# A graph network's steady loop: a new table of due times, and the output bias moved from TensorE to GpSimd

## The chip, the cores and the metric

The kernel runs on one core of a Trainium2 chip. Its engines work beside each other, each through its own list of instructions in a fixed order, and wait for each other by semaphores: TensorE (PE, with its weight loads listed as PEld), VectorE (DVE), ScalarE (ACT), GpSimd (POOL) and SyncE (SP), which issues the transfers. The metric is the device time of one execution in microseconds (us); of several runs the median is taken.

## The reference

Two layers over 128 graphs of 128 nodes with 64 features, each followed by a residual addition and a layer norm. Layer 0 sums a relu over the edges that exist, layer 1 is a dense product with the adjacency followed by three small linear layers.

```python
# layer 0
mask = (adj > 0.0).astype(x.dtype)
h = relu((x @ W1a)[:, :, None, :] + (x[:, :, None, :] - x[:, None, :, :]) @ W1b + b1)
hm = einsum('bjkh,bjk->bjh', h, mask)
x = layernorm(x + hm @ W2 + mask.sum(-1)[..., None] * b2)
# layer 1
h = elu(einsum('bmn,bnd->bmd', adj, x) @ V1 + c1)
h = elu(h @ V2 + c2)
x = layernorm(x + h @ V3 + c3)
```

H is 192 in layer 0, 128 in layer 1; about 6% of the adjacency is nonzero.

## The kernel before

Two graphs make a pair; there are 64 pairs, and every step below works on one pair. The nodes of a graph are sorted by degree, so that nodes with few edges stand together. The sorted nodes fall into nine blocks (`BLOCKS`), each with a number of slots that no node of the block is expected to exceed. For each block, a *unit* computes the edge sums: ACT fills a PSUM bank with the node's own term (L910, "fill"), PE adds the neighbours' terms through a one-hot matrix `oh` (18 matmuls at L920, "gather"), DVE sums absolute values over the slots (L930, "reduce"). Four PSUM banks (`edges`) serve the units in turn. A second path, at the end of the program, handles pairs with too many edges; no instruction of it appears among the costly groups.

Before its units a pair is prepared. `prepare` counts degrees (DVE L545), forms keys (POOL L552, L553), spreads them over the partitions (PE L248, "spread") and ranks the nodes (DVE L568, L575). `turn` transposes inputs (PE L690, L691; ACT L695). `project_c` forms the neighbours' projection in three bf16 parts, `cp` (PE L708, L711; ACT L718; DVE L722; ACT L725; POOL L727). `sort_x` and `project_a` sort the features and form the own term `aj` (PE L592 "x sort", L606 "projection a"; ACT L613), and a correction `corr` (POOL L620 `sa`; PE L626, L629 "short rows"; DVE L635 `ea`; POOL L642). `sort_mask` sorts the mask (PE L246 "mask sort"; ACT L659, L661), takes prefix sums ("vps"; ACT L668) and writes the one-hot matrices, nine per pair (DVE L675).

After its units a pair is finished by `finish`: POOL `hm` (L842), PE "project" (L847, L851), ACT `ys` (L855), PE "unsort" (L864), then `norm`, giving `x1` (DVE L737 addition and L742 statistics; POOL L749, L750, L753, called "fac1" here; ACT L771), PE "aggregate" (L871), ACT `agg` (L875), PE "hidden1" (L880), `elu` (ACT r L791, e L794; DVE h L797), PE "hidden2" (L886), `elu` again, PE "last" (L891 and L893), and `norm` again ("fac2" is its POOL part), giving `o`, which SP writes out (L897). In the old kernel L891 adds the bias row `c3` by a matmul of ones with `rowp`, in which the row stands as three bf16 parts, in front of the two products L893 that accumulate onto it. The row was centred when it was prepared (`consts_late`, a chain of some twenty small DVE operations, L508 to L366), since the norm subtracts the mean.

What order the instructions stand in is decided when the program is built, by `Flow`. Each activity above is a thread, a list of steps, and each step has a due time: `ROUND` times the pair's number plus an entry of `DUE`. At first, `Flow.run` issues whatever its cost estimates say can start earliest. From the first fill on (`flow.under_way`), and until the last 14 units, it issues in strict order: of all threads whose next step has its inputs issued and PSUM banks free, the one with the smallest due time. Apart from units, the other steps share four further PSUM banks, handed out in the order in which they were given back. The due times thus are ranks: they set the order on every engine, and no engine ever passes an instruction that waits. Where PE changes between full-array matmuls and tiled ones the planner also distinguishes modes (`PE:t` two column halves, `PE:r` two row halves, `PE:x` transposes).

Of the kernel before, what the change touches and what calls it, by code (L numbers as in the profile page):

```python
# [31 lines left out]
F32 = mybir.dt.float32  # L32
# [154 lines left out]
def sparse(tc, env):  # L187

    g = type("env", (), dict(env))
    nc, P, N, F, H, O, HB, H1, NP, E = (  # L190
        g.nc, g.P, g.N, g.F, g.H, g.O, g.HB, g.H1, g.NP, g.E)
# [7 lines left out]
    EV = {}  # L199


    ROUND = 11.1651
    AHEAD = 4

    DUE = {
        "prepare": (-42.67, -37.79, -37.67, -37.41, -37.15),
        "sort_x": (-21.11, -18.03, -15.85, -13.03, -12.9, 2.76, 2.89, 3.02, 3.14),
        "sort_mask": (-28.04, -27.66, -27.27, -15.21, -14.95, -14.31, -14.05, -13.8, -13.54,
                      -13.28, -3.02, -2.76, -2.5, -2.25),
        "turn": (-38.05, -37.92),  # L210
        "project_c": (-31.63, -29.71, -29.58, -29.45, -29.32, -17.13, -13.15),
        "finish": (12.51, 20.73, 21.24, 21.37, 21.5, 21.88, 22.01, 27.91, 28.3, 28.68, 32.02,
                   34.97, 35.1, 35.23, 41.26, 41.39, 43.95, 44.08, 46.78, 46.91, 54.48, 54.61,
                   59.48),
        "unit": [(0.06, 0.19, 0.32), (0.83, 0.96, 1.09), (0.45, 0.58, 0.71), (2.37, 2.5, 2.63),
                 (3.27, 3.4, 3.53), (4.43, 4.56, 4.68), (4.81, 4.94, 5.07), (5.33, 5.71, 6.1),
                 (7.64, 10.97, 11.1)],
    }

    def begin_thread(name, p, gen):  # L220
# [2 lines left out]
    def event(*key):  # L223
        return EV.setdefault(key, [])

    def happened(ev, *key):
        event(*key)[:] = ev
# [8 lines left out]
    def dve(n):  # L236
        return 0.08 + n / 960
# [12 lines left out]
    def flat(t):  # L250
        return t.rearrange("p s n -> p (s n)")
# [48 lines left out]
    rows = temp([P, NR], F32, "rows")  # L300
# [16 lines left out]
    def made(*names):  # L317
        return [event("const", name) for name in names]
# [410 lines left out]

    LATE = NP - 1  # L730

    def norm(p, yps, ev, name, rest, shift):


        y = work.tile([P, 2, O], F32, name="y", bufs=6)
        ev, = yield ("DVE", dve(2 * O), [ev], 0,
                     lambda: nc.vector.tensor_add(flat(y), yps[:, :2 * O], flat(rest)))  # L737
        flow.give(yps, ev)
        st = work.tile([P, 2, 3], F32, name="st", bufs=12)

        ev, = yield ("DVE", 0.2, [ev], 0,
                     lambda: nc.vector.bn_stats(st.rearrange("p s t -> p (s t)"),  # L742
                                                y.rearrange("p s f -> p f s")))
        ve = work.tile([P, 2], F32, name="ve", bufs=12)
        rs = work.tile([P, 2], F32, name="rs", bufs=12)
        nb = work.tile([P, 2], F32, name="nb", bufs=12) if shift else None

        def factors():
            nc.gpsimd.tensor_scalar(ve, st[:, :, 2], 1.0 / F, EPS, op0=OP.mult, op1=OP.add)  # L749
            nc.gpsimd.tensor_tensor(rs, ve, mhalf, op=OP.pow)  # L750
            if shift:
                for s in range(2):
                    nc.gpsimd.tensor_scalar(nb[:, s:s + 1], st[:, s, 1:2], rs[:, s:s + 1], -1.0,  # L753
                                            op0=OP.mult, op1=OP.mult)

        def variance():
            nc.vector.tensor_scalar(ve, st[:, :, 2], 1.0 / F, EPS, op0=OP.mult, op1=OP.add)

        def center(s):
            nc.vector.tensor_scalar(o[:, s, :], y[:, s, :], st[:, s, 1:2] if shift else 0.0,  # L760
                                    rs[:, s:s + 1], op0=OP.subtract, op1=OP.mult)
        if p < LATE:
            ev, = yield ("POOL PORT", 1.27 if shift else 0.97, [ev] + made("mhalf"), 0, factors)
        else:
            ev, = yield ("DVE", 0.1, [ev], 0, variance)
            ev, = yield ("POOL", 0.7, [ev] + made("mhalf"), 0,
                         lambda: nc.gpsimd.tensor_tensor(rs, ve, mhalf, op=OP.pow))
        o = work.tile([P, 2, F], F32, name=name, bufs=6)

        def apply(s):  # L770
            nc.scalar.activation(o[:, s, :], y[:, s, :], AF.Identity,  # L771
                                 bias=nb[:, s:s + 1] if shift else 0.0, scale=rs[:, s:s + 1])
        if p < LATE:
            ev, = yield ("ACT", 0.6 if shift else 0.46, [ev], 0, lambda: [apply(s) for s in range(2)])
        elif shift:
            ev, = yield ("DVE", 0.4, [ev], 0, lambda: [center(s) for s in range(2)])
        else:

            have = ev
            ev, = yield ("ACT", 0.3, [have], 0, lambda: apply(0))  # L780
            evv, = yield ("DVE", 0.2, [have], 0, lambda: center(1))
            ev = [max(ev[0], evv[0])] + ev[1:] + evv[1:]
        return o, ev
# [18 lines left out]
    def overflow():  # L802
# [29 lines left out]
        ev, = yield ("DVE", 0.2, [ev], 0, lambda: v.tensor_reduce(some, t[:1, :B], AX.X, OP.max))  # L832
        flow.give(t, ev)

    def finish(p):

        d, xx = S[p], XX[p]
        hm = work.tile([P, 3, N], F32, name="hm")
        late = p >= LATE
        ev, = yield ("DVE PORT" if late else "POOL PORT", 0.47 if late else 1.05,  # L840
                     [event("corr", p)] + [event("sums", p, i) for i in range(NB)], 0,
                     lambda: (nc.vector if late else nc.gpsimd).tensor_sub(hm, d["sums"], d["corr"]))  # L842

        def project(yb):
            cp, mtp = d["cp"], d["mtp"]
            for c in range(3):
                nc.tensor.matmul(yb[:, :2 * O], hm[:, c, :], flat(w2d[:, c]),  # L847
                                 start=(c == 0), stop=False)
            for s in range(2):
                for i in range(3):  # L850
                    nc.tensor.matmul(yb[:, s * O:(s + 1) * O], mtp[:, s, :], cp[:, i, s, H:H + O],  # L851
                                     start=False, stop=(s == 1 and i == 2))
        ev, yb = yield ("PE", 0.85, [ev] + made("w2d"), 1, project)
        ys = work.tile([P, 2 * O], F32, name="ys")
        ev, = yield ("ACT", act(2 * O), [ev], 0, lambda: nc.scalar.copy(ys, yb[:, :2 * O]))  # L855
        flow.give(yb, ev)
        if p == NP - 1:
            due = DUE["finish"]
            flow.start(ROUND * p, [due[4]] * 4 + [due[8], due[12], due[12], due[14], due[15], due[15]],
                       overflow())  # L860

        def unsort(t):
            for s in range(2):
                nc.tensor.matmul(t[:, s * O:(s + 1) * O], d["permT"][:, s, :],  # L864
                                 ys[:, s * O:(s + 1) * O], start=True, stop=True)
        ev, t = yield ("PE", 0.4, [ev, event("permT", p)], 1, unsort)
        x1, ev = yield from norm(p, t, ev, "x1", xx, True)

        def aggregate(t):
            for s in range(2):  # L870
                nc.tensor.matmul(t[s * F:(s + 1) * F, :N], x1[:, s, :], d["turned"][:, s, :],  # L871
                                 start=True, stop=True)
        ev, t = yield ("PE:t", 0.22, [ev, event("turned", p)], 1, aggregate)
        agg = work.tile([P, N], F32, name="agg")
        ev, = yield ("ACT", act(N), [ev], 0, lambda: nc.scalar.copy(agg, t[:, :N]))  # L875
        flow.give(t, ev)

        def hidden1(zb):
            for s in range(2):
                nc.tensor.matmul(zb[:, s * N:(s + 1) * N], v1p[:, s, :], agg,  # L880
                                 start=True, stop=True)
        ev, zb = yield ("PE", 0.49, [ev] + made("v1p"), 1, hidden1)
        h1, ev = yield from elu(zb, ev, "h1", 0)

        def hidden2(zb):
            nc.tensor.matmul(zb[:, :2 * N], v2s, h1, start=True, stop=True)  # L886
        ev, zb = yield ("PE", 0.48, [ev], 1, hidden2)
        h2, ev = yield from elu(zb, ev, "h2", 1)

        def last(t):  # L890
            nc.tensor.matmul(t[:, :2 * O], onesb[:, :P], c3p, start=True, stop=False)  # L891
            for s in range(2):
                nc.tensor.matmul(t[:, s * O:(s + 1) * O], h2[:, s * N:(s + 1) * N], v3s,  # L893
                                 start=False, stop=(s == 1))
        ev, t = yield ("PE", 0.51, [ev] + made("rowp", "v3s"), 1, last)
        o, ev = yield from norm(p, t, ev, "o", x1, False)
        nc.sync.dma_start(g.out[2 * p:2 * p + 2].rearrange("b j f -> j b f"), o)  # L897


# [279 lines left out]
```

## Time and profile before

| what | value |
|---|---|
| median of 3 runs | 772.05 us (771.89 to 772.5) |
| the profiled execution | 772.32 us |
| its span, first to last instruction | 770.6 us |
| PE busy | 746.3 us (97%), 14616 matmuls |
| DVE busy | 725.2 us (94%) |
| ACT busy | 705.5 us (92%) |
| POOL busy | 430.1 us (56%) |
| mean granted clock of PE | 0.985 |
| one pair in the steady part (381.72 to 393.11) | 11.39 us |

A group of instructions is listed by its line, engine and operation, with what it writes and reads, the number of instructions, the busy time, and the mean duration of one in ns. A wait is listed as the waiting engine and instruction, what released it, and the total, the number and the longest of its times in us. A stage is given as its limits in us from the span's start, its length, and the busy time of each engine (with the number of instructions), then the granted clock, the busy share of the DMA engines and GB/s. In a timeline the first number is the start, the second the time to the end of the last instruction of the row. Matmuls overlap, so what one costs PE is read from start to start.

### The profile page before, as it was taken

How to read it: one execution, taken by the hardware profiler on the slowest of the kernel's cores; microseconds unless marked ns; L12 is line 12 of the kernel's file. 1: busy time of each engine (PE TensorE's matmuls, PEld its weight loads, DVE VectorE, ACT ScalarE, POOL GpSimd, SP SyncE). 2: the span in 40 equal slices, each digit the busy share in tenths (PEclk: the TensorE clock that was granted, in tenths of full speed). 3: DMA queues.
4: the chain of work that ended last, by engine and by line, in shares of the span. 5: the costliest groups of instructions: out<-in, count | busy, mean ns of one | idle time of the engine just before them, and what ended most of it. 6: DMA issues, size and time to landing. Idle time of an engine off the chain costs nothing.

```text
span 770.6 us, 36007 instructions
## 1 busy us (share of the span) xinstructions
PE 746.3 (97%) x14616; PEld 679.5 (88%) x14617; DVE 725.2 (94%) x2381; ACT 705.5 (92%) x1986; POOL 430.1 (56%) x801
## 2 busy tenths in 40 slices
PE   7599999999999999999999999999999999999995
PEld 5489999999999999999999999999999999999993
DVE  6699999999999999999999999999999999999994
ACT  5479999999999999999999999999999999999984
POOL 5145565565565565556556556556555655655652
PEclk9699999999999999999999999999999999999997
DMA  4000010110110011011011011011101101100000
GB/s 123 11 3 3 17 30 17 30 31 20 27 30 23 24 31 30 16 31 30 17 30 30 17 30 31 21 26 31 30 17 30 31 16 31 31 17 19 11 10 21
DMA packets 54668, 19.70 MB, mean 26 GB/s; under 512 B 37601, under 2 KB 54497, under 8 KB 54497
## 3 DMA queue, kind: packets, MB, share of 16 engines
q1 hardware_dynamic: 53792, 17.05, 9.1%
q8 instruction: 116, 1.90, 1.0%
q14 instruction: 56, 0.45, 0.2%
q10 hardware_dynamic: 704, 0.30, 0.2%
HBM read 13.14 MB, written 4.19 MB: 22 GB/s over the span
## 4 chain that ended last, share of the span: by engine, by line
PE 94%; DVE 3%; ACT 2%; issue 0%; DMA 0%; POOL 0%; ACTq 0%; POOLq 0%; DVEq 0%
PE e L920 45%; PE m L606 6%; PE m L708 5%; PE m L847 5%; PE m L880 4%; PE m L886 4%; PE m L864 4%; PE m L893 4%; PE m L690 3%; PE m L248 2%; PE m L871 2%; PE m L592 2%; PE m L246 2%; PE m L851 1%; PE m L711 1%; PE m L691 1%
## 5 line engine op out<-in xcount | busy, mean ns | idle before, releaser
L920 PE MATMUL e<-oh,cp 128*64 128x162 bf16 (+3 forms) x10368 | 392.7, 229 | 6.2 <-DVE oh L675 5.2
L920 PEld LDWEIGHTS <-cp 128*64 128x64 bf16 x10368 | 356.9, 110 | 15.3 <-issue 6.9
L930 DVE TENSOR_REDUCE sums<-e 128x54 f32<-128x486 f32 (+8 forms) x576 | 327.1, 609 | 16.7 <-PE m L629 9.9
L910 ACT COPY e<-aj 128x504 f32<-128x504 f32 (+6 forms) x576 | 293.3, 540 | 9.5 <-DVE sums L930 8.9
L749 POOL TENSOR_SCALAR ve<-st 128x2 f32<-128x2 f32 x126 | 24.1, 191 | 254.1 <-DVE st L742 246.9
L675 DVE TENSOR_TENSOR oh<-vp,slotc 128x308 bf16<-128x308 bf16 (+6 forms) x576 | 137.3, 314 | 0.8 <-ACT vp L668 0.6
L750 POOL TENSOR_TENSOR rs<-ve,mhalf 128x2 f32<-128x2 f32 x126 | 87.8, 696 | 10.5
L727 POOL TENSOR_TENSOR cp<-r,cp 128x512 bf16<-128x512 f32 x64 | 74.4, 1162 | 18.6 <-ACT cp L725 18.6
L642 POOL TENSOR_TENSOR corr<-ea,sa 128x384 f32<-128x384 f32 x64 | 64.2, 1003 | 32.8 <-DVE ea L635 32.8
L842 POOL TENSOR_TENSOR hm<-sums,corr 128x384 f32<-128x384 f32 x63 | 63.1, 1002 | 5.8 <-DVE sums L930 5.8
L620 POOL TENSOR_TENSOR sa<-aj,srow 128x384 f32<-128x384 f32 x64 | 65.4, 1021 | 0.0
L797 DVE SCALAR_TENSOR_TENSOR h<-m,cc,e 128x256 f32<-128x256 f32 x128 | 60.8, 475 | 3.8 <-ACT e L794 3.6
L791 ACT ACTIVATE r<-m,cc 128x256 f32<-128x256 f32 x128 | 61.3, 479 | 2.4 <-PE m L886 2.4
L606 PEld LDWEIGHTS m<-xsT,wad 128*128 128x128 f32 x384 | 48.3, 193 | 13.0 <-ACT turned L695 11.8
L613 ACT ACTIVATE aj<-m,b1c 128x128 f32<-128x128 f32 x192 | 57.2, 386 | 2.3 <-PE m L606 2.3
L606 PE MATMUL m<-xsT,wad 128*128 128x128 f32 x384 | 58.4, 289 | 0.6 <-DVE r L722 0.6
L794 ACT ACTIVATE e<-r 128x256 f32<-128x256 f32 x128 | 53.3, 418 | 2.0
L847 PE MATMUL m<-w2d,hm 128*128 128x128 f32 x384 | 53.4, 276 | 0.0
L722 DVE TENSOR_TENSOR r<-m,cp 128x256 f32<-128x256 f32 x128 | 47.8, 415 | 2.8 <-ACT cp L718 2.8
L771 ACT ACTIVATE x<-y,nb,rs 128x64 f32<-128x64 f32 x126 | 48.9, 439 | 1.4 <-POOL nb L753 1.4
L847 PEld LDWEIGHTS m<-w2d,hm 128*128 128x128 f32 x384 | 48.1, 192 | 0.1
L708 PE MATMUL m<-wc,turned 64*128 64x256 f32 x256 | 46.3, 436 | 0.9 <-DVE r L722 0.9
(159 smaller groups left out, 1350.5 us busy)
## 6 DMA issues: line engine op xcount, KB each, us to landing
adj<-in_adj_dram SPq DMA_DIRECT2D x64, 128.0 KB, 2.4
xx<-in_x_dram SPq DMA_DIRECT2D x64, 64.0 KB, 2.2
out_dram<-o SPq DMA_DIRECT2D x64, 64.0 KB, 1.6
w1s<-in_L_gnn_W_dram ACTq DMA_DIRECT2D x2, 96.0 KB, 2.8
w2s<-in_L_gnn_W_dram ACTq DMA_DIRECT2D x2, 48.0 KB, 2.7
v2s<-in_L_gnn_W_dram SPq DMA_DIRECT2D x1, 64.0 KB, 2.3
v1d<-in_L_gnn_W_dram SPq DMA_DIRECT2D x2, 32.0 KB, 2.0
rows<-in_L_gnn_b_dram SPq DMA_DIRECT2D x1, 64.0 KB, 4.8
```

Source lines behind the costliest of these rows:

```text
L606: nc.tensor.matmul(aps[:, c * N:(c + 1) * N], wad[:, c, :], xsT, start=True, stop=True)
L620: evs, = yield ("POOL PORT", 1.0, [have] + made("srow"), 0, lambda: nc.gpsimd.tensor_mul(sa, aj, srow))
L642: ev, = yield ("POOL PORT", 1.05, [ev, evs], 0, lambda: nc.gpsimd.tensor_sub(corr, ea, sa))
L675: lambda: nc.vector.tensor_tensor(oh[:, :, c].rearrange("p b (s w) -> p b s w", w=w), vp[:, :, p0:p1].rearrange("p b (o w) -> p b o w", o= ...
L708: nc.tensor.matmul(cps[s][:, :cols], d["turned"][k, 2, :], wc[k, :], start=True, stop=False)
L727: lambda: nc.gpsimd.tensor_sub(cp[:, 2], r1, cp[:, 1]))
L750: nc.gpsimd.tensor_tensor(rs, ve, mhalf, op=OP.pow)
L842: lambda: (nc.vector if late else nc.gpsimd).tensor_sub(hm, d["sums"], d["corr"]))
L847: nc.tensor.matmul(yb[:, :2 * O], hm[:, c, :], flat(w2d[:, c]), start=(c == 0), stop=False)
L910: lambda: nc.scalar.copy(e.rearrange("p (c s w) -> p c s w", c=3, w=w), d["aj"][:, :, p0:p1].rearrange("p c (o w) -> p c o w", o=1) .to_br ...
L920: nc.tensor.matmul(e[s * HB:(s + 1) * HB, c * n:(c + 1) * n], cp[:, k, s, c * HB:(c + 1) * HB], oh[:, s, base:base + n], start=False, stop ...
L930: nc.vector.tensor_reduce(d["sums"][:, :, p0:p1], e.rearrange("p (c s w) -> p c w s", c=3, w=w), AX.X, OP.add, apply_absolute_value=True)
```

## The change

The table `DUE` and the length `ROUND` are replaced, which reorders every engine. Units come about 11 us earlier in it relative to all else: preparation begins 32.8 us ahead of the first unit of a pair (before: 42.7), and the output is due 44.4 us after the last gather (before: 48.5). `AHEAD`, the number of pairs loaded ahead, stays 4. The bias row is no longer added by PE: a new thread `residual` has POOL add the f32 row `rows` to `x1`, into a new tile `x1c` with four buffers, and the last norm's addition on DVE takes `x1c` where it took `x1`, and waits for it. The matmuls L893 start their own accumulation.

```diff
-    ROUND = 11.1651
+    ROUND = 11.2051
     AHEAD = 4

     DUE = {
-        "prepare": (-42.67, -37.79, -37.67, -37.41, -37.15),
-        "sort_x": (-21.11, -18.03, -15.85, -13.03, -12.9, 2.76, 2.89, 3.02, 3.14),
-        "sort_mask": (-28.04, -27.66, -27.27, -15.21, -14.95, -14.31, -14.05, -13.8, -13.54,
-                      -13.28, -3.02, -2.76, -2.5, -2.25),
-        "turn": (-38.05, -37.92),
-        "project_c": (-31.63, -29.71, -29.58, -29.45, -29.32, -17.13, -13.15),
-        "finish": (12.51, 20.73, 21.24, 21.37, 21.5, 21.88, 22.01, 27.91, 28.3, 28.68, 32.02,
-                   34.97, 35.1, 35.23, 41.26, 41.39, 43.95, 44.08, 46.78, 46.91, 54.48, 54.61,
-                   59.48),
-        "unit": [(0.06, 0.19, 0.32), (0.83, 0.96, 1.09), (0.45, 0.58, 0.71), (2.37, 2.5, 2.63),
-                 (3.27, 3.4, 3.53), (4.43, 4.56, 4.68), (4.81, 4.94, 5.07), (5.33, 5.71, 6.1),
-                 (7.64, 10.97, 11.1)],
+        "prepare": (-43.98, -43.85, -38.06, -37.93, -37.29),
+        "sort_x": (-30.98, -27.11, -26.98, -24.02, -21.32, -21.19, -8.95, -8.82, -8.69),
+        "sort_mask": (-27.76, -27.63, -27.5, -25.69, -25.57, -25.31, -25.05, -24.79, -14.23,
+                      -13.97, -13.72, -12.43, -12.17, -11.91),
+        "turn": (-35.87, -35.74),
+        "project_c": (-29.82, -29.69, -29.56, -29.43, -29.3, -26.6, -16.81),
+        "finish": (1.35, 9.21, 9.34, 9.72, 10.11, 10.37, 10.63, 14.88, 17.45, 17.58, 22.09,
+                   23.89, 24.15, 24.41, 26.85, 26.98, 27.11, 27.24, 31.88, 32.26, 37.03, 37.16,
+                   44.37),
+        "residual": (22.4,),
+        "unit": [(-10.75, -10.63, -10.5), (-11.14, -11.01, -10.88), (-9.6, -9.34, -9.08),
+                 (-8.44, -8.31, -8.18), (-7.92, -6.12, -5.99), (-8.05, -5.86, -5.73),
+                 (-6.25, -3.93, -3.8), (-5.47, -3.54, -3.41), (-4.06, -0.19, -0.06)],
     }
...
-    def norm(p, yps, ev, name, rest, shift):
+    def norm(p, yps, ev, name, rest, shift, *after):
...
-        ev, = yield ("DVE", dve(2 * O), [ev], 0,
+        ev, = yield ("DVE", dve(2 * O), [ev, *after], 0,
                      lambda: nc.vector.tensor_add(flat(y), yps[:, :2 * O], flat(rest)))
...
+    def residual(p, x1, x1c, ev):
+
+        ev, = yield ("POOL PORT", 0.45, [ev] + made("rows"), 0,
+                     lambda: nc.gpsimd.tensor_add(flat(x1c), flat(x1), rows))
+        happened(ev, "x1c", p)
...
         x1, ev = yield from norm(p, t, ev, "x1", xx, True)
+        x1c = work.tile([P, 2, F], F32, name="x1c", bufs=4)
+        flow.start(ROUND * p, DUE["residual"], residual(p, x1, x1c, ev))
...
         def last(t):
-            nc.tensor.matmul(t[:, :2 * O], onesb[:, :P], c3p, start=True, stop=False)
             for s in range(2):
                 nc.tensor.matmul(t[:, s * O:(s + 1) * O], h2[:, s * N:(s + 1) * N], v3s,
-                                 start=False, stop=(s == 1))
+                                 start=True, stop=True)
         ev, t = yield ("PE", 0.51, [ev] + made("rowp", "v3s"), 1, last)
-        o, ev = yield from norm(p, t, ev, "o", x1, False)
+        o, ev = yield from norm(p, t, ev, "o", x1c, False, event("x1c", p))
```

## The prediction

> **What bounds the kernel now.** I read the page first (who is busy), then the busy time in the stages of the span (which part of the span the change can touch), then the waits of TensorE, then the timeline of one round. Stages, with the granted clock before the DMA share:
>
> ```profile
> core 0: us, PE busy (x) PEld busy (x) DVE busy (x) ACT busy (x) POOL busy (x), PEclk, DMA share, GB/s
> 18.50:25.00 6.50, 4.74 (x26) 3.43 (x22) 3.13 (x11) 2.34 (x6) 1.66 (x2) 0.65 0.18 43
> 25.00:31.00 6.00, 1.08 (x10) 0.64 (x10) 5.51 (x25) 2.29 (x7) 0.45 (x1) 0.50 0.00 0
> 31.00:38.00 7.00, 5.83 (x116) 5.18 (x113) 3.47 (x7) 3.83 (x10) 0.98 (x1) 0.78 0.00 0
> ```
>
> ```profile
> 381.72:393.11 11.39, 11.39 (x229) 10.45 (x229) 11.07 (x37) 10.97 (x32) 6.63 (x12) 1.00 0.11 26
> 393.11:404.50 11.39, 11.39 (x229) 10.46 (x228) 11.07 (x37) 10.97 (x32) 6.62 (x12) 1.00 0.11 27
> ```
>
> Two regimes. In the steady one a pair takes 11.39 us, repeated to 0.01; PE has no gap, DVE and ACT are 97% busy. In the head, up to about 45 us, PE waits and its clock falls to half. The waits of PE, longest first, are almost all from head and tail:
>
> ```profile
> PE e L920 <- DVE oh L675: 5.2, 2, 4.9
> PE m L893 <- DVE h L797: 2.2, 2, 1.4
> ```
>
> So a steady round costs what PE's instructions take from start to start; a producer matters only once it is late. The timeline of PE around the removed row:
>
> ```profile
> 384.08 0.70 PE L708 MATMUL m<-wc,turned 64*128 64x256 f32 x4
> 384.71 0.23 PE L711 MATMUL m<-b2p,onesb 128*128 128x64 bf16 x2
> 384.78 0.22 PE L891 MATMUL m<-rowp,onesb 128*128 128x128 bf16 x1
> 384.84 0.61 PE L893 MATMUL m<-v3s,h 128*128 128x64 f32 x4
> 385.38 0.29 PE L920 MATMUL e<-oh,cp 128*64 128x112 bf16 x4
> ```
>
> The bias row's record lasts 0.22 but the next starts 0.06 later: 0.06 is its price.
>
> **What the Trainium skill says.** TensorE: Matmul & The Clock Gate (Wait — 56ns, not 53.3ns?) gives 55.6 ns from start to start for 128 warm columns; the trace's 0.06 agrees. Its section What's actually happening says that an idle PE is clocked at half until busy again; the 0.50 at 25 to 31 us agrees. TensorEngine Tiling (Array Packing), Key Properties: changing the tiling mode drains TensorE. The trace agrees: the unsort (L864) takes 0.58 before a tiled gather (381.14 to 381.72) and 0.47 before an untiled step (745.02 to 745.49), 0.11 a change. SBUF — State Buffer, Who interferes with whom: a VectorE operation with two SBUF inputs and a GpSimd one that reads SBUF exclude each other. L675 is one; in the round shown POOL ends 389.65 and the nine L675 run 391.13 to 393.18, so this trace shows no collision.
>
> **The change, part by part.** The planner, once the first fill is out, always issues the thread with the smallest due time, so sorting each table modulo its round gives the order per engine; done on the table before, it gives the trace's PE order exactly. For the new table PE has, from gather 8 on: gathers 8, 1, 0, 2, short rows, gather 3, projection c, hidden2, gathers 4, 5, mask sort, aggregate, x sort, spread, gathers 6, 7, vps, turn, project, last, projection a, unsort, hidden1.
>
> (1) Bias row gone from PE: 0.06 a round.
>
> (2) PE order. Old and new have the same six mode changes a round (tiled, row-tiled, untiled, tiled, transpose, untiled, tiled again), so no drain is won in number; they only sit behind other steps. From start to start, old to new: last 0.54 to 0.55 (the change after it goes, but its first weights now follow the 64-column matmuls of project; hidden1, which followed them before, took 0.53 where four records of about 0.107, as L847 has them, are 0.43: 0.10 for that place); hidden2 0.49 to 0.60 (a change behind it now); aggregate 0.33 to 0.22 and vps 0.11 to 0.21 (the change to transpose moves from one to the other); unsort 0.58 to 0.47; hidden1 0.53 to 0.54 (0.10 less ahead, 0.11 for the change behind). Sum old 2.58, new 2.59: 0.01 lost, an estimate good to 0.06 either way. Gathers, sorts and the rest keep their tiled neighbours and their times. With (1): 0.05 a round.
>
> (3) Stalls from the new order. I laid the engines' orders end to end with the old trace's start-to-start times, and 0.06 for a handover (aggregate ends 389.35, its copy starts 389.40); on the old order this gives ACT a wait of 0.18 at L659 and POOL one of 0.51 at L642, and the list of waits has 9.6/55 = 0.17 and 32.8/63 = 0.52. On the new one, from the start of gather 8: hidden2 is reached after 0.67+0.29+0.64+0.66+0.11+0.46+0.70 = 3.53. Its h1 on DVE stands behind reduces 8, 1, 0 and the count: gather 0 ends at 0.67+0.29+0.64+0.17 = 1.77, reduce 0 runs 1.83 to 2.40, count 0.41, h1 0.48, handover 0.06: 3.35. Slack 0.18, where the old order had over 4 us. The spread (PE at 6.09) takes the PSUM bank that h2 frees: hidden2 ends 4.2, r2 0.48, e2 0.42 after it, h2 behind two L722 on DVE until 6.03: late by 0 to 0.06. Fill 3 precedes gather 3 by 0.14, old 1.07. Everything else has over 0.2 (x1 to aggregate 1.6, ys to unsort 0.66, hm to project 2.9). Price: 0 to 0.06, kept at 0 because PE's own pitch in (2) is as uncertain; late next would be h1 and hidden2. DVE loses one old wait (permute directly after rank, 0.11): now reduce 6 stands between. DVE's 11.07 a round keep it under PE's 11.34, barely.
>
> (4) POOL's addition, 128x128 f32. Not in the old trace; POOL takes 0.31 for 128x64 (L363) and 1.00 for 128x384 (L842), on the line between 0.31 + 64 x 0.0022 = 0.45. It stands after fac1 and before keys, sa, hm, corr, fac2, cp2. POOL was idle 3.9 before L749, so 64 x 0.45 = 29 us vanish there; I take nothing, since y2 needs it 8 us later. Bounds: nothing, or 1.0 a round. Laid out, POOL's chain ends at 8.3 and L675 starts at 9.2: cover 0.9. Were it gone, cp2 (1.16) would hold L675 or be held, and DVE with 0.3 spare would push PE by up to 0.9. The wait added to y2's L737 (DVE; behind it oh 6, y1, oh 7, bn1) is long met.
>
> (5) Pairs in flight. Preparation begins 32.8 us before the units instead of 42.7. Loads follow unit starts as before: issued over a round ahead (11 us old: 385.67 to 396.6) for 2.4 us of landing; on SP they still queue behind an output that waits for its `o` (SP waits there 623 us in 56 times, 11 us each, also before the change); nothing. Buffers live shorter; x1c's four hold one round. Free.
>
> (6) Head. In 18.50 to 44.8 PE did about 12 us of work (gathers of pair 0 and three of pair 1: 6.9; three projections c 2.1; two a 1.5; rest 1.5), so 14 us were lost, part to the half clock. DVE did 18.4 of 26.3. The reason: units' due times lay after nearly all preparation of pairs 0 to 2 and after the 4.6 us chain of late constants on DVE (24.1 to 28.7); the L675 of both pairs came after it at 28.7. Now units are due 11 us earlier, before the chain (due -5.6, after gather 5), so gathers should start about 20 to 21 rather than 25.4 and 30.7. The chain then falls into round 0 and holds reduce 6 instead. DVE bounds the gain: 26.3 - 18.4 = 7.9. Below it can be nothing, or -2 if PE cools again behind the chain. I take half, 4.0.
>
> (7) Tail. From the last gather's end (749.3) to 770.6 it is one pair's chain; it loses one bias row and POOL's addition is beside it. 0, within 1.5.
>
> Sum over the 58 rounds outside head and tail: 58 x 0.05 = 2.9; with 4.0, 6.9. The profiled execution took 772.3 with a span of 770.6; 772.3 - 6.9 = 765.4, and the median of the runs lies 0.3 below it: **765**.
>
> **Rivals.** A, same time (770.5 to 773.6): mode changes and the 0.06 stall eat (1), and the chain merely moves within the head: 772.05 - 58 x 0.02 = 771, with the head at 0. For: PE's wash in (2). Against: PE idle for 4.9 in one wait that the order made. B, slower: DVE's h1, with slack 0.18, and the bank from h2 turn into a wait of each round. It decides when a round stalls by more than 6.9/58 = 0.12. At 0.2: 765 + 58 x 0.2 = 777; at 0.3: 782. I give it as 777. For: DVE at 97%, handovers of 0.14 exist (L635 to L642), slack gone from 4 to 0.18. Against: hidden2 and spread are the only such links. C, much faster: PE never cools, head gains 7, drains come out well, 0.11 a round: 772 - 7 - 58 x 0.11 = 758.6. For: DVE bound of 7.9; against: DVE at 11.07 - 0.11 = 10.96 leaves no room for waits.
>
> **Chances.** Forecast (760 to 770.5) 0.43, C (below 760) 0.15, A 0.10, B 0.32. Range 755 to 779: it leaves out the far ends of B and C. The forecast's own is 760 to 770.5. Faster by over 0.2% 0.58, within it 0.10 (1.5 us, about what a measurement of this kernel can tell), slower 0.32.
>
> **What would show it.** Right: a round of 11.28 to 11.40 with no PE gap; L891 gone; first long gather near 21 us; a POOL group of 64 at 0.45. Wrong: PE waits at L886 for DVE h or at L248 for a bank, times 60; L675 longer than 0.34 or POOL's cp beside it; the first gathers still near 30 us.

## The result and the profile after

| | before | after |
|---|---|---|
| median of 5 runs each, same chip | 772.50 us (771.89 to 772.95) | 768.38 us (767.67 to 768.54) |
| ratio, 95% interval | | 0.9947 [0.9932, 0.9961] |
| the profiled execution | 772.32 | 767.67 |
| its span | 770.6 | 765.9 |
| one pair in the steady part | 11.39 | 11.26 |
| mean granted clock of PE | 0.985 | 0.981 |

Faster by 4.1 us, where 6.9 was forecast. In the listing of the changed kernel the lines behind the table stand one further down (L675 is L676), those after 833 seven to nine (L920 is L928, `hidden1` is L889, `hidden2` L895, `last` L901); POOL's addition is L839.

The sum hides three larger numbers. I mark each kernel by the start of the first long gather of a pair ("gather 8", 128x170), and cut the span into what lies before that of pair 4, the 55 rounds from there to pair 59, and what follows:

| | up to pair 4 | pairs 4 to 59 | from pair 59 to the end | span |
|---|---|---|---|---|
| before | 85.45 | 626.71 | 58.44 | 770.6 |
| after | 82.54 | 619.66 | 63.70 | 765.9 |
| difference | -2.9 | -7.05 | +5.3 | -4.7 |

So the steady rounds won more than twice what was forecast, the head somewhat less, and the tail, put at nothing, gave 5.3 back. The stages of the head and one round, in the view of busy time by stage, kernel after (the granted clock is the number before the DMA share):

```profile
core 0: us, PE busy (x) PEld busy (x) DVE busy (x) ACT busy (x) POOL busy (x), PEclk, DMA share, GB/s
18.50:25.00 6.50, 3.74 (x45) 2.99 (x45) 4.07 (x12) 4.26 (x11) 0.99 (x1) 0.61 0.17 43
25.00:31.00 6.00, 6.00 (x116) 5.36 (x113) 4.61 (x13) 3.23 (x9) 2.12 (x2) 0.85 0.01 3
31.00:38.00 7.00, 3.23 (x69) 2.60 (x64) 6.58 (x25) 3.65 (x10) 1.10 (x1) 0.93 0.00 1
38.00:44.80 6.80, 6.22 (x94) 5.34 (x95) 4.34 (x11) 2.72 (x7) 3.11 (x3) 0.57 0.02 4
386.59:397.85 11.26, 11.26 (x232) 10.23 (x231) 10.99 (x37) 10.86 (x33) 7.05 (x13) 1.00 0.11 27
```

The hole has moved, not gone: at 25 to 31 us PE is now full, at 31 to 38 it works 3.23 of 7.00, and in the stage after that the clock is 0.57. The waits of PE, kernel after, longest first:

```profile
PE e L928 <- DVE oh L676: 4.4, 2, 2.6
PE m L895 <- DVE h L798: 4.1, 3, 1.5
PE e L928 <- ACT e L918: 1.7, 1, 1.7
```

The wait of 4.9 for the one-hot matrices has become two that sum to 4.4 (the longest 2.6), with one of 1.7 for a fill beside them; and `hidden2` waits 4.1 in three times, all in the tail. No wait is listed 58 times; the stalls of each round that rival B feared did not come. The timeline of PE at the end of a steady round, kernel after:

```profile
394.83 0.83 PE L854 MATMUL m<-w2d,hm 128*128 128x128 f32 x6
395.50 0.34 PE L858 MATMUL m<-cp,mtp 128*128 128x64 bf16 x6
395.67 0.64 PE L901 MATMUL m<-v3s,h 128*128 128x64 f32 x4
396.14 0.89 PE L607 MATMUL m<-xsT,wad 128*128 128x128 f32 x6
396.87 0.56 PE L871 MATMUL m<-ys,permT 128*128 128x64 f32 x4
397.26 0.66 PE L889 MATMUL m<-agg,v1p 128*128 128x128 f32 x4
397.85 0.26 PE L928 MATMUL e<-oh,cp 128*64 128x170 bf16 x2
```

From start to start: `last` 0.47, projection a 0.73, unsort 0.39, hidden1 0.59.

### The profile page after: what moved, and what is told of

It is laid out like the page before. It is cut to its first block, busy times and chain, and to the rows that moved or that the text cites. A ratio compares the mean times of both kernels' runs of the same rounds, so it can differ in the third digit from the quotient of the medians.

```text
span 765.9 us, 36061 instructions
## 1 busy us (share of the span) xinstructions
PE 740.0 (97%) x14790; PEld 667.8 (87%) x14791; DVE 719.7 (94%) x2381; ACT 700.1 (91%) x1986; POOL 458.7 (60%) x865
## 4 chain that ended last, share of the span: by engine, by line
PE 94%; DVE 2%; ACT 1%; DMA 0%; issue 0%; POOL 0%; ACTq 0%; POOLq 0%; DVEq 0%
PE e L928 46%; PE m L607 6%; PE m L854 6%; PE m L709 5%; PE m L895 4%; PE m L889 4%; PE m L901 4%; PE m L247 4%; PE m L871 3%; PE m L691 3%; PE m L880 2%; PE m L593 2%; PE m L858 1%; PE m L712 1%; PE m L692 1%; DVE oh L676 1%
## 5 line engine op out<-in xcount | busy, mean ns | idle before, releaser
L928 PE MATMUL e<-oh,cp 128*64 128x66 bf16 (+3 forms) x10368 | 383.9, 229 | 6.2 <-DVE oh L676 4.4
L928 PEld LDWEIGHTS <-cp 128*64 128x64 bf16 x10368 | 348.3, 111 | 34.5 <-issue 26.4
L938 DVE TENSOR_REDUCE sums<-e 128x9 f32<-128x198 f32 (+8 forms) x576 | 339.8, 609 | 21.6 <-PE e L928 19.3
L676 DVE TENSOR_TENSOR oh<-vp,slotc 128x308 bf16<-128x308 bf16 (+6 forms) x576 | 154.3, 314 | 0.9 <-ACT vp L669 0.8
L792 ACT ACTIVATE r<-m,cc 128x256 f32<-128x256 f32 x128 | 61.5, 481 | 6.1 <-PE m L889 4.5
L795 ACT ACTIVATE e<-r 128x256 f32<-128x256 f32 x128 | 54.9, 429 | 2.1
L607 PEld LDWEIGHTS m<-xsT,wad 128*128 128x128 f32 x384 | 48.5, 194 | 1.5 <-DVE r L723 1.0
L895 PE MATMUL m<-h,v2s 128*128 128x256 f32 x128 | 44.0, 426 | 4.1 <-DVE h L798 4.1
```

The source lines that it names most:

```text
L607: nc.tensor.matmul(aps[:, c * N:(c + 1) * N], wad[:, c, :], xsT, start=True, stop=True)
L676: lambda: nc.vector.tensor_tensor(oh[:, :, c].rearrange("p b (s w) -> p b s w", w=w), vp[:, :, p0:p1].rearrange("p b (o w) -> p b o w", o= ...
L928: nc.tensor.matmul(e[s * HB:(s + 1) * HB, c * n:(c + 1) * n], cp[:, k, s, c * HB:(c + 1) * HB], oh[:, s, base:base + n], start=False, stop ...
L938: nc.vector.tensor_reduce(d["sums"][:, :, p0:p1], e.rearrange("p (c s w) -> p c w s", c=3, w=w), AX.X, OP.add, apply_absolute_value=True)
```

## The experiments

Three questions stood open: why the round won 0.13 and not 0.05 (is it the bias row, the mode changes, or something that the old order made PE wait for?), what holds the head, and what lengthens the tail. Three letters in the expectations stand for theories that run through several of them: **W**, the old order made PE wait for `ys` before the unsort without the profile listing it; **M**, what counts is which steps stand at the changes of mode; **H**, the chain of late constants on DVE holds the head. Every kernel was timed side by side with the kernel before, and its ratio is taken to that.

### The two halves of the change

*The new table alone*, the bias row left on PE and the last norm taking `x1`:

```diff
-        flow.start(ROUND * p, DUE["residual"], residual(p, x1, x1c, ev))
+            nc.tensor.matmul(t[:, :2 * O], onesb[:, :P], c3p, start=True, stop=False)
-                                 start=True, stop=True)
+                                 start=False, stop=(s == 1))
-        o, ev = yield from norm(p, t, ev, "o", x1c, False, event("x1c", p))
+        o, ev = yield from norm(p, t, ev, "o", x1, False)
```

> The new due times with the bias row still added on TensorE (matmul of ones with the row ahead of the last products). Theory T, read from the two traces: a steady round fell by 0.13 us (11.39 to 11.26), 0.06 of it the bias row and 0.07 the new order of TensorE's steps. Then the round here is 11.32 and the time 768.4 + 60 x 0.06 = 772, within 1 us of before. Rival R1, the bias row is all of the gain and the table is neutral: round 11.39, 772.5. Rival R2, the table is all of it: round 11.26, 768.4. Time alone does not part T from R1; the round does.

Measured: 767.78, ratio 0.9956 [0.9942, 0.9969]; round 11.29 (383.93 to 395.22).

*The bias on POOL alone*, under the old table and `ROUND`, with the addition due at 31.72:

```diff
-        "finish": (1.35, 9.21, 9.34, 9.72, 10.11, ...
-        "residual": (22.4,),
+        "finish": (12.51, 20.73, 21.24, 21.37, 21.5, ...
+        "residual": (31.72,),
```

> The old due times with the bias row added by GpSimd (its addition due after cp's third part, where GpSimd stands idle, and before the one-hot block on VectorE). T: round 11.33, the ends as before, 772.5 - 60 x 0.06 = 768.9. R1: the same, 768.4. R2, the table is all of the gain: 772.5. If the addition on GpSimd or the wait for it costs anything, the round is above 11.33.

Measured: 772.72, ratio 1.0015 [1.0008, 1.0021]; round 11.36. PE in its timeline:

```profile
384.23 0.64 PE L901 MATMUL m<-v3s,h 128*128 128x64 f32 x4
384.80 0.64 PE L928 MATMUL e<-oh,cp 128*64 128x112 bf16 x18
```

`last` takes 0.57 here, where row and `last` together took 0.60 before (384.78 to 385.38). Under both tables the row is worth 0.03 a round, half of the 0.06 from its start to the next start: without it the first weights of `last` have nothing to load behind (before, they load from 384.78 on, beside the row). Over 58 rounds that is 1.7, and the end takes it back: from pair 59 on it is 61.6 with the old table and the bias on POOL (58.4 before), and 63.7 after against 61.4 with the new table alone. These are one profile each, and the first is of an execution 1.5 us above its median; the medians do not show a gain from the bias row either (under the old table 772.72 against 771.75 for the kernel before; under the new one a ratio of 0.9947 with the bias on POOL and of 0.9956 without). The new table gives all of the gain in time that can be told from none: 11.39 to 11.29 a round.

### Which step of the new order wins

*hidden1 ahead of the unsort*, in the changed kernel; the order of those two is the only thing moved on PE:

```diff
-        "finish": (1.35, 9.21, 9.34, 9.72, 10.11, 10.37, 10.63, 14.88, 17.45, 17.58, 22.09,
+        "finish": (1.35, 9.21, 9.34, 9.72, 10.11, 10.37, 10.63, 14.88, 17.45, 17.58, 20.85,
```

> The changed kernel with one due time moved, so that hidden1 comes ahead of unsort and unsort stands directly before a tiled gather again, as in the kernel before. T, the place of a mode change sets what the short-streaming steps cost: unsort and hidden1 take 0.53 + 0.58 = 1.11 in place of 0.39 + 0.59 = 0.98, round 11.39, time 768.4 + 58 x 0.13 = 776. Rival, only the number of mode changes counts and this is the same: round 11.26, 768.4.

Measured: 777.62, ratio 1.0079 [1.0066, 1.0093]; round 11.43. The two steps do not get dearer: hidden1 0.45 and unsort 0.49, 0.94 where the changed kernel has 0.98. The loss is elsewhere. The wait list of DVE between 300 and 600 us:

```profile
DVE y L738 <- PE m L871: 10.8, 27, 0.4
```

Each round DVE stands 0.40 at y1, which needs the unsort that now comes later, and the last one-hot matrices are queued behind it. The next four gathers take 2.45, from the start of the first to the start of what follows, where the changed kernel has 2.27. PE is not listed as waiting in them. But the third gather goes on only at 392.50, after 0.23 between two matmuls that elsewhere in it are at most 0.07 apart, and the last one-hot ends at 392.45. That PE waits for it is inferred from these times; the next run tests it.

*The same, with y1 and its statistics put behind the last one-hot:*

```diff
-        "finish": (1.35, 9.21, 9.34, 9.72, 10.11, 10.37, 10.63, 14.88, 17.45, 17.58, 22.09,
+        "finish": (1.35, 9.21, 9.34, 9.72, 10.53, 10.54, 10.63, 14.88, 17.45, 17.58, 20.85,
```

> As hidden1_first, and y1 and its statistics on VectorE moved behind the last one-hot matrix, so that VectorE no longer waits for unsort in front of it (0.40 a round there, and gather 0 thinned out until that matrix was done). Theory W, unsort next to a tiled gather costs no more than elsewhere when ys is early (0.45 + 0.49 for hidden1 and unsort in the two runs that had it, 0.98 in the changed kernel, 1.11 in the kernel before): round 11.20 to 11.27, 766 to 769. Theory M, the place of the mode change costs: round 11.36 or more, 774 or more.

Measured: 766.28, ratio 0.9925 [0.9913, 0.9938]; round 11.21. PE in its timeline:

```profile
384.49 0.61 PE L889 MATMUL m<-agg,v1p 128*128 128x128 f32 x4
384.93 0.56 PE L871 MATMUL m<-ys,permT 128*128 128x64 f32 x4
385.42 2.44 PE L928 MATMUL e<-oh,cp 128*64 128x170 bf16 x72
387.68 0.23 PE L627 MATMUL m<-srow,small 128*64 128x128 bf16 x2
```

hidden1, then the unsort, then a tiled gather: the old order of these three, with `ys` long ready. They take 0.44 and 0.49, 0.93 together, and the gathers 2.26. Before, the same three steps took 0.53 and 0.58. The timelines of PE and of ACT, kernel before:

```profile
380.61 0.69 PE L880 MATMUL m<-agg,v1p 128*128 128x128 f32 x4
381.14 0.65 PE L864 MATMUL m<-ys,permT 128*128 128x64 f32 x4
381.72 0.48 PE L920 MATMUL e<-oh,cp 128*64 128x170 bf16 x8
```

```profile
380.00 0.89 ACT L613 ACTIVATE aj<-m,b1c 128x128 f32<-128x128 f32 x3
380.81 0.27 ACT L855 COPY ys<-m 128x128 f32<-128x128 f32 x1
```

Two different things make up this difference of some 0.17. The weight loads of the two steps tell them apart. First the kernel before, then this run:

```profile
380.58 0.53 PEld L880 LDWEIGHTS m<-agg,v1p 128*128 128x128 f32 x4
381.13 0.52 PEld L864 LDWEIGHTS m<-ys,permT 128*128 128x128 f32 x4
```

```profile
384.38 0.53 PEld L889 LDWEIGHTS m<-agg,v1p 128*128 128x128 f32 x4
384.82 0.53 PEld L871 LDWEIGHTS m<-ys,permT 128*128 128x128 f32 x4
```

From the first load of hidden1 to the first of the unsort it is 0.546 before and 0.446 here. Before, `ys` ends at 381.08 and the unsort's first weights load at 381.13. So PE stood for `ys` in every round, for 0.10, and no wait is listed, because the modelled end of hidden1 (381.30) covers the gap. It shows in the unsort's 0.58 instead of 0.49. The 0.08 of hidden1 is no wait but its place: behind the 64-column matmuls of project its first matmul starts 0.03 after its first load (380.61), behind projection a 0.11 after it (384.49), and what is counted to hidden1 in one order is counted to the step ahead of it in the other. W stands, at about 0.10 a round, which is what the new table alone gave; M falls, since the unsort stands at the same change of mode here, and the round is 11.21, below the changed kernel's 11.26.

*The old table with `ys` made earlier*, W's own remedy, in the kernel before:

```diff
-        "finish": (12.51, 20.73, 21.24, 21.37, 21.5, 21.88, 22.01, 27.91, 28.3, 28.68, 32.02,
+        "finish": (12.51, 20.44, 20.46, 21.37, 21.5, 21.88, 22.01, 27.91, 28.3, 28.68, 32.02,
```

> The kernel before with two due times moved: project goes ahead of projection a on TensorE, and ys ahead of aj on ScalarE, so that a whole projection stands between project and unsort. Mode changes, bias row and depth stay as before. Theory W, formed on the last runs: what the new order saved is a wait of unsort for ys that the list of waits does not show, since the modelled ends of hidden1 cover it (ys ends 381.08, unsort's first weights load at 381.13, and hidden1 and unsort take 0.53 + 0.58 there against 0.45 + 0.49 where ys is early). Then the round falls from 11.39 to 11.22 to 11.28 and the time to 763 to 766. Rival M, the place of the mode changes made the difference: round 11.39, 771.8.

Measured: 790.34, ratio 1.0234 [1.022, 1.0248]; round 11.62: the expectation missed by 24 us. ACT and PE in its timeline:

```profile
385.75 0.27 ACT L855 COPY ys<-m 128x128 f32<-128x128 f32 x1
386.50 0.89 ACT L613 ACTIVATE aj<-m,b1c 128x128 f32<-128x128 f32 x3 [0.48 <-PE m L606]
387.27 0.42 ACT L794 ACTIVATE e<-r 128x256 f32<-128x256 f32 x1
387.57 1.10 ACT L910 COPY e<-aj 128x486 f32<-128x486 f32 x2
```

```profile
386.30 0.61 PE L880 MATMUL m<-agg,v1p 128*128 128x128 f32 x4
386.75 0.56 PE L864 MATMUL m<-ys,permT 128*128 128x64 f32 x4
387.24 2.75 PE L920 MATMUL e<-oh,cp 128*64 128x170 bf16 x72
389.91 0.70 PE L708 MATMUL m<-wc,turned 64*128 64x256 f32 x4
```

hidden1 and unsort take 0.45 and 0.49. But project, now behind hidden2, takes 0.74 for 0.67: projection a, project, hidden1 and unsort together take 2.60 (384.64 to 387.24) where they took 2.69 (390.42 to 393.11), so the wait was worth 0.09 and not the 0.17 that the expectation reckoned with. And project, moved ahead, pushed projection a behind it: ACT waits 0.48 for it in every round, and, with only the 0.4 to spare that it had before, then hands its fills over late. The four gathers take 2.67 instead of 2.36 (the third stands until 388.21, its fill ends at 388.16). So W is right that PE waited and wrong in how cheaply the wait goes: made earlier, `ys` hands it to ACT. In the new table ACT copies `ys` as soon as project ends (395.87) and has an output and two fills to do before `aj` (397.27).

### The head

*Constants spread*: in the changed kernel the steps of the late constants' chain are due 1.2 us apart, so that they stand between DVE's other work instead of ahead of it all:

```diff
-    flow.start(ROUND * -0.5, [0.0], consts_late())
+    flow.start(ROUND * -0.5, [0.0] * 4 + [1.2 * k for k in range(1, 19)], consts_late())
```

> The changed kernel with the chain of late constants on VectorE given due times 1.2 us apart (from -5.6 to 16) in place of one due time for all. Theory H: in the changed kernel the chain (30.35 to 34.1) stands in front of the one-hot matrices of pair 1 and stops TensorE for 1.8 and 2.6 us, after which its clock is at half. Then gather 8 of pair 1 comes at 44 to 46 in place of 49.55 and the time is 763 to 766. Rival: VectorE's sum of work bounds the head, and spreading moves the same work: 767.5 to 769.

Measured: 764.72, ratio 0.991 [0.9895, 0.9925]. Why, in the changed kernel's own timelines, first PE, then DVE (the chain runs from L509 to L367; its middle is left out):

```profile
32.67 0.86 PE L928 MATMUL e<-oh,cp 128*64 128x170 bf16 x18
35.28 0.73 PE L928 MATMUL e<-oh,cp 128*64 128x66 bf16 x19 [1.75 <-ACT e L918]
38.58 1.24 PE L928 MATMUL e<-oh,cp 128*64 128x162 bf16 x15 [2.58 <-DVE oh L676]
```

```profile
30.35 0.14 DVE L509 TENSOR_TENSOR cc<-cc,m 128x1 f32<-128x1 f32 x1
...
33.96 0.18 DVE L367 COPY rowp<-low 1x128 bf16<-1x128 bf16 x1
34.18 1.23 DVE L938 TENSOR_REDUCE sums<-e 128x39 f32<-128x507 f32 x2
35.44 0.78 DVE L676 TENSOR_TENSOR oh<-vp,slotc 128x224 bf16<-128x224 bf16 x3
```

The chain holds DVE from 30.35 to 34.14, then come the reductions that it delayed, which free the banks of the fills, and only then the one-hots of pair 1. PE stands twice, 4.3 together, and cools. In the spread kernel one wait is left there, and the view by stage has the clock at 1.00 in both stages:

```profile
35.69 1.46 PE L928 MATMUL e<-oh,cp 128*64 128x162 bf16 x35 [1.71 <-DVE oh L676]
```

```profile
31.00:38.00 7.00, 5.29 (x132) 4.72 (x126) 6.63 (x21) 5.19 (x13) 2.43 (x2) 1.00 0.02 5
38.00:44.80 6.80, 6.80 (x137) 6.24 (x135) 6.80 (x26) 5.77 (x17) 2.12 (x2) 1.00 0.01 2
```

Gather 8 of pair 4 starts at 78.94 instead of 82.54, and the span is 3.8 shorter: the chain in one piece, delay and cold clock together, costs 3.6 more than the chain spread out. H stands.

*One round more of preparation*: units, finish, residual and the late constants all 11.2051 later, prepare, sorts and projections as they are. The order of the steady loop is the same (one round is added to all of them), but one pair more is in flight:

```diff
-        "unit": [(-10.75, -10.63, -10.5), (-11.14, -11.01, -10.88), (-9.6, -9.34, -9.08),
+        "unit": [(0.4551, 0.5751, 0.7051), (0.0651, 0.1951, 0.3251), (1.6051, 1.8651, 2.1251),
...
-    flow.start(ROUND * -0.5, [0.0], consts_late())
+    flow.start(ROUND * 0.5, [0.0], consts_late())
```

> The changed kernel with units, finishing, the bias addition and the chain of late constants due one round (11.2051) later against preparation: the same order on every engine in a steady round, with one more pair in preparation. T, depth only moves work between the ends (before and after differ by 2.9 us less in the head and 5.2 us more in the tail): round 11.26, head longer by 2 to 5 us, tail shorter by about as much, 768.4 within 2. Rival, fewer pairs in flight is itself what helps: 771 or more, with a longer round or a longer head. Other rival, the shallow depth is what costs the tail 5 us and the head gains little: 765 or less.

Measured: 764.48, ratio 0.9907 [0.9892, 0.9922]; round 11.26. The first gather comes later (25.5 instead of 21.3), yet pair 4's at 81.69, 0.85 earlier, and the last part takes 61.5 instead of 63.7. Having fewer pairs in flight thus costs 3.9 by the two medians (3.2 with each set against the kernel before that was timed beside it), at both ends.

*Two rounds more*, as above with 22.4102 and five pairs loaded ahead:

```diff
-    AHEAD = 4
+    AHEAD = 5
-    flow.start(ROUND * -0.5, [0.0], consts_late())
+    flow.start(ROUND * 1.5, [0.0], consts_late())
```

> As deeper, by two rounds instead of one, with five pairs loaded ahead in place of four: same order in a steady round. Theory D, more preparation in flight takes preparation out of the last rounds, where TensorE would otherwise hold units back, and costs the head less than that: another 1 to 4 us, 760 to 763. Rival, one round was enough to bring the one-hot matrices of pair 1 ahead of the chain of constants, and more only lengthens the head: 765 to 770.

Measured: 770.12, ratio 0.9969 [0.9957, 0.998]; round 11.26. Pair 4's gather 8 at 89.36, 7.7 later than with one round more; the last part 59.5, 2.0 shorter. Each round of depth buys about 2 us of tail; the first costs the head nothing, the second, with five pairs loaded ahead, 7.7.

*One round more and the constants spread:*

```diff
+        "unit": [(0.4551, 0.5751, 0.7051), (0.0651, 0.1951, 0.3251), (1.6051, 1.8651, 2.1251),
...
+    flow.start(ROUND * 0.5, [0.0] * 4 + [1.2 * k for k in range(1, 19)], consts_late())
```

> As deeper, and the chain of late constants spread by 1.2 us a step as in spread. If the two gained by the same thing (the one-hot matrices of pair 1 no longer behind the chain), it is 763.5 to 765; if deeper gained in the tail (its gathers end sooner) and spread in the head, the sum of both, 760 to 762.

Measured: 765.42, ratio 0.9906 [0.9891, 0.992]: no sum of the two gains. Pair 4's gather 8 is at 83.73, later than with either alone (one profile, of an execution 1.4 us above its median). In the deeper kernel the chain no longer makes PE wait for one-hots, so there is nothing of that kind for the spreading to save. Its constants then seem only to fall into rounds in which DVE is the bound: between 44.8 and 60 us DVE is busy for 15.06 of 15.20 and PE for 12.30, where one round more alone has PE at 15.20.

### The tail

*Keeping PE warm*: twenty added matmuls of 512 columns in the last pair's finish, their results unused:

```diff
+            if p == NP - 1:
+                for k in range(6):
+                    nc.tensor.matmul(edges[k % NE], identb, d["oh"][:, 0, :512], start=True, stop=True)
```

> The changed kernel with 20 matmuls of 512 columns, into PSUM banks that no unit needs any more, in the last pair's finish: 6 after unsort, 2 after aggregate, 6 after hidden1, 6 after hidden2, each 0.21 us at full clock, so that TensorE is busy where it waits. Theory C: from about 750 us TensorE's clock is at half because it waits, and the last pair's aggregate, hidden1, hidden2 and last take 0.4 to 0.6 us longer each: 766 to 767. Rival: the added matmuls delay the chain as much as the clock gains, or the clock stays low: 768.4 or more.

Measured: 767.87, ratio 0.994 [0.9926, 0.9954]; span 766.3 against 765.9, so no gain to be seen. Of the last steps, in the changed kernel's timeline of PE:

```profile
755.23 1.22 PE L895 MATMUL m<-h,v2s 128*128 128x256 f32 x2 [1.53 <-DVE h L798]
757.99 1.11 PE L901 MATMUL m<-v3s,h 128*128 128x64 f32 x4 [1.53 <-DVE h L798]
```

and in this kernel's (`hidden2` is L904, `last` L913 there):

```profile
756.53 0.70 PE L904 MATMUL m<-h,v2s 128*128 128x256 f32 x2
758.76 0.66 PE L913 MATMUL m<-v3s,h 128*128 128x64 f32 x4 [0.24 <-DVE h L798]
```

The two steps shrink by 0.5 each, as the half clock would have it (the Trainium skill, TensorE: Matmul & The Clock Gate, What's actually happening; 0.50 is also the granted clock of the changed kernel's last 13 us). But `last` of pair 62 had moved from 746.71 to 747.65 and the last aggregate from 750.79 to 751.67, both behind the added matmuls, which ate it. The cold clock alone is not what makes this tail longer than that of before, whose last `hidden2` and `last` are also cold (1.22 and 1.12).

### POOL's cover

*The addition four times over*, the same result each time, so as to use up the cover of 0.9 that the prediction named:

```diff
-                     lambda: nc.gpsimd.tensor_add(flat(x1c), flat(x1), rows))
+                     lambda: [nc.gpsimd.tensor_add(flat(x1c), flat(x1), rows) for k in range(4)])
```

> The changed kernel with GpSimd's addition done four times over (3 x 0.46 = 1.4 us more a round, the same result). The prediction's step 4 said that the addition is free as long as GpSimd's chain ends 0.9 us ahead of the one-hot block on VectorE. If so, 1.4 exceeds the cover by 0.5: the third part of cp runs into the one-hot block, a round of 11.4 to 11.8 and 776 to 800. If GpSimd is free altogether (no exclusion between the two, and nobody waits for it): round 11.26, 768.4.

Measured: 777.87, ratio 1.0081 [1.0068, 1.0095]; round 11.41. The timelines of POOL and of DVE in it:

```profile
381.20 2.06 POOL L839 TENSOR_TENSOR x1c<-x,rows 128x128 f32<-128x128 f32 x4
...
387.49 1.16 POOL L728 TENSOR_TENSOR cp<-r,cp 128x512 bf16<-128x512 f32 x1
```

```profile
388.04 1.88 DVE L676 TENSOR_TENSOR oh<-vp,slotc 128x224 bf16<-128x224 bf16 x6
```

In the changed kernel POOL's last operation ends 0.64 ahead of DVE's block of one-hots (395.10 and 395.74). Three more additions (1.6) push it to 388.65, 0.6 into the block. The block takes 1.88 instead of 1.40, the longest single L676 between 300 and 600 us 777 ns instead of 342, and DVE is busy 11.31 of the 11.41. That POOL and an operation of DVE with two SBUF inputs exclude each other (the Trainium skill, SBUF — State Buffer, Who interferes with whom) agrees with the 0.48. Done once, the addition costs the steady round nothing; four times, it makes the run 9.5 us longer.

### The two best together

*One round more, and hidden1 ahead of the unsort with y1 behind the last one-hot:*

```diff
-        "finish": (1.35, 9.21, 9.34, 9.72, 10.11, 10.37, 10.63, 14.88, 17.45, 17.58, 22.09,
+        "finish": (12.5551, 20.4151, 20.5451, 20.9251, 21.7351, 21.7451, 21.8351, 26.0851, 28.6551, 28.7851, 32.0551,
...
-    flow.start(ROUND * -0.5, [0.0], consts_late())
+    flow.start(ROUND * 0.5, [0.0], consts_late())
```

> Preparation one round earlier and hidden1 ahead of the unsort with y1 behind the last one-hot, together. The first change alone measured 764.5, the second 766.3, against 768.4 for the change as it is. Theory (the ends and the steady round are separate: the first edit acts on where the first and the last pairs fall, the second on every round): the steady round is 11.21, as with the second edit alone, and the gains add: 764.5 - 58 x 0.05 = 761.6, within 0.8, with gather 8 of pair 59 about 3 us earlier than the 701.0 that the first edit alone gave. Rival (what one of them wins another limit takes, as with the spread constants, where the DVE of the first rounds became the bound): the round is 11.21 all the same, but the first gathers come later or the tail longer, and the time stays at 764 to 766.

Measured: 760.49, ratio 0.9865 [0.9841, 0.9888]; round 11.21. The two do not take from each other, and the version beats both kernels: against the change as it is they gain 3.9 and 2.1 alone, and 7.9 together. That they more than add comes from the end: with the order alone the part from pair 59 on is 64.85, with both it is 59.87; why was not tried. Gather 8 of pair 59 is at 698.53, 2.5 earlier than with the depth alone. All spans, cut as at the beginning:

| | up to pair 4 | pairs 4 to 59 | from pair 59 to the end | span |
|---|---|---|---|---|
| new table alone | 82.14 | 621.27 | 61.39 | 764.8 |
| bias on POOL alone | 85.67 | 625.09 | 61.64 | 772.4 |
| hidden1 first | 82.54 | 629.29 | 64.07 | 775.9 |
| hidden1 first, y1 later | 82.81 | 616.74 | 64.85 | 764.4 |
| old table, `ys` early | 85.16 | 639.02 | 64.42 | 788.6 |
| constants spread | 78.94 | 619.59 | 63.57 | 762.1 |
| one round more | 81.69 | 619.30 | 61.51 | 762.5 |
| two rounds more | 89.36 | 619.14 | 59.50 | 768.0 |
| one more, spread | 83.73 | 619.30 | 61.97 | 765.0 |
| PE kept warm | 82.18 | 619.66 | 64.46 | 766.3 |
| addition four times | 82.29 | 627.37 | 66.44 | 776.1 |
| one more, hidden1 first | 82.11 | 616.42 | 59.87 | 758.4 |

## Why the prediction was right, and where not

The side was right, and the size within the range of the likeliest case, 768.4 for 765. But that close a size was luck: two steps were off by about 4 and 5 us in opposite directions.

**(1) The bias row**, 0.06 a round: mis-sized. It is 0.03 under either table, since its matmul covered part of the first weight load of `last`. From start to start was read right; what the next instruction would do without the row was not asked.

**(2) The order of PE "a wash, 0.01 lost"**: this step failed; the order won 0.10. By its own items, predicted and measured: hidden2 0.60 and 0.61, aggregate 0.22 and 0.23, vps 0.21 and 0.21, so the mode changes did move as it said, and they are the wash that it took them for. But `last` is 0.47 for 0.55, unsort 0.39 for 0.47, hidden1 0.59 for 0.54. The unsort's old 0.58 was read as the price of the step and its mode change; 0.09 to 0.10 of it was the wait for `ys` that no view lists, and which the new order ends. `last` was charged 0.10 for a new place behind 64-column matmuls, but it stood behind such matmuls (L711) in the old order too: it takes 0.57 there without the row and with a mode change behind it, 0.47 now without one. And hidden1 was let off all of the 0.10 of its old place, while behind the unsort some 0.05 of it stays. The price of a change, 0.11, came out near all the same: the unsort is 0.49 ahead of a tiled gather and 0.39 ahead of hidden1.

**(3) Stalls**: held. From gather 8, hidden2 starts at 3.63 (3.53 laid out) and h1 ends at 3.36 (3.29): with the handover of 0.06 a slack of 0.21 where 0.18 was reckoned; no wait for a bank is listed. Of the mechanism of rival B, a DVE late in each round, the order of y1 (11.43) and four additions (11.41) show that it was near: both cost 0.15 to 0.17 a round.

**(4) POOL's addition**: held, 0.459 for 0.45. The cover is 0.64 where 0.9 was laid out, and using it up delays the one-hots, as was said.

**(5) Fewer pairs in flight, "free"**: held for the steady round (11.26 at every depth), wrong at the ends. The step asked only about buffers and loads. One round more is worth 3.2 to 3.9.

**(6) The head**, 4.0 of at most 7.9: mis-sized, 2.9. Gathers start at 21.3 as said. The step saw that the chain would now fall into round 0 and let it hold reduce 6 alone; it also held the one-hots of pair 1 and the reductions that free the fills' banks, and PE cooled, which had been only the bound below. Spread out, the head gains 6.5 against before (85.45 to 78.94), near the bound of 7.9.

**(7) The tail**, 0 within 1.5: this step failed; it cost 5.3. It looked only past the last gather, whose end is at 749.50 and not 749.3; from there the tail grew from 21.1 to 23.3. The other 3.1 lie before that: from pair 59's gather 8 to the end of the last gather it is 37.3 before and 40.4 after. Before, the next pitches shrink (pairs 59 to 60 10.89, 60 to 61 9.98), since preparation runs out a round earlier there; after they are 11.26 and 10.81, and with one round more 10.81 and 9.15. Less depth leaves more work to the end. One round more gives 2.2 back. The bias on POOL has a like share, 2.3 to 3.2 by one profile each, and some 1.5 to 2.6 at both ends together by the medians; why the planner's order of the last 14 units comes out longer with it was not tried and stays open.

So 6.9 was -2.9 in rounds and -4.0 in the head; the trace has -7.05, -2.9 and +5.3, 4.7 of span. Rival A, the mode changes as the limit, fell. Rival C came near in its size of the round's gain (0.11, where 0.13 was measured) and in nothing else.

## What to carry to other kernels

A start-to-start time is a price only when nothing was waited for: compare the first weight load of a step with the end of what it reads on the producer's timeline, in particular where the profile lists no wait. It also belongs to a step and its neighbours: before a difference is called a gain, add up all the steps of the stretch, since one step's 0.08 can be another's. When a table of due times shifts one stage against another, cost both ends as well as the round: the depth that the steady state does not need shortens the last rounds, and what the shift moves into the first rounds is queued ahead of something. Two gains can add if they act in different parts of the span (depth and the order within a round: 760.5), not if they remove the same wait (depth and spread constants: 765.4).

## What was not expected of the hardware

- A matmul of 128 bf16 columns that starts 0.06 ahead of f32 ones is worth 0.03 when removed (`last` 0.57 alone, 0.60 with it; 0.47 and 0.50 under the new table).
- Waits of 0.1 to 0.3 us can stand in every round without being listed: the unsort's for `ys` (0.10), and in the kernel with `ys` early 0.31 over four gathers.
- What a step of f32 weights costs from start to start depends on the step ahead: hidden1 takes 0.53 behind the 64-column matmuls of project and 0.45 behind projection a, and project 0.67 behind projection a and 0.74 behind hidden2.
- An idle PE pays for long after the wait: in the changed kernel waits of 1.7 and 2.6 us between 33 and 39 us are followed by a clock of 0.57 over 38 to 44.8 us, with PE busy for 6.22 of 6.80.
